# A table set with Exp and Ln loaded by the kernel in a selective scan layer, and two buffers for a norm's row of variances

## The chip, the cores and the metric

The kernel runs on one core of a Trainium2 chip, in one launch. The metric is the device time of the launch in microseconds; a kernel is given by the median of its runs. A profile records one execution with the start and the duration of every instruction. The engines are TensorE (PE, its weight loads as PEld), VectorE (DVE), ScalarE (ACT), GpSimd (POOL) and SyncE (SP), which issues the DMAs. Each takes its own instructions in order.

ScalarE evaluates functions such as Exp, Ln, Silu and Sqrt from tables. The tables come in sets, one set is active at a time, and the instruction that makes another set active shows in the profile as ACT_TABLE_LOAD, under the line of the instruction that it stands in front of.

## The reference

Four layers follow each other on x of shape (8, 64, 64, 64). The change touches the first, a visual state-space block. Cut to what matters, for each of 8 images with 4096 positions and 128 inner channels:

```python
xh = xh + _ss2d(_ln(xh, ...), ...)

def _ss2d(x, ...):
    xi, z = split(x @ in_proj_w.T + in_proj_b)
    xc = silu(_dwconv3(xi, conv_w, conv_b))
    # four directions k: rows, columns, and both reversed
    dts, Bs, Cs = split(xs @ xproj_w)
    dts = softplus(dts @ dtproj_w + dtproj_b)
    # per channel and state n of 16:
    #   h = h * exp(dt * A) + dt * B * u ;  y = sum_n h * C
    y = _ln(y, outnorm_g, outnorm_b) * silu(z)
    return y @ outproj_w.T + outproj_b
```

`_ln` is (x - u) * rsqrt(v + eps) * g + b with mean u and variance v over the channels. The layers after it (a gate with two attentions, a modifier that is trained for two steps, and a last attention) are not changed.

## The kernel before

**Tiling.** Channels lie on the 128 partitions, positions along the free axis. An image is cut into 4 chunks of 1024 positions for the scan (`CH`) and 8 blocks of 512 for everything else (`BK`). `scan_layer` goes over 8 images, and in each over 16 steps: 4 directions times 4 chunks. A step has 16 turns, one for each state n.

**A turn.** The order is written out by hand (a manual schedule), in program order for each engine. For state n, with the work for later states interleaved:

- `decay` (L733, ACT): a = Exp(dt * A_n), two turns ahead, three buffers;
- `spread` (L743 to L754): the row B_n into a PSUM tile z. For 12 of the 16 states PE does it (L751), and DVE multiplies z by dt * u (L778). For the states 0, 3, 6 and 8 (`BY_POOL`) a DMA brings B_n broadcast into `bt`, POOL multiplies (L741), and ACT copies the product to z (L748);
- the scan h = a * h + z on DVE (L782);
- ct = C_n * h on POOL (L787), where ct came by a broadcast DMA (L729, five buffers);
- two turns later, PE adds ct to the sum over n in PSUM (L848); ACT copies the sum of a whole step out (L817);
- ACT copies the last column of h to the state for the next chunk (L769).

**Background work.** Everything that isn't the scan itself stands in a queue of items (`Background`). A turn takes one item: `before` runs its PE half (`make`) and `after`, at the end of the next turn, its other half (`use`), mostly an ACT instruction that empties the PSUM bank. DMAs that such an item ends in are put off to the following turn (`later`). The items: the input norm and projection for the next image, a gate (Silu at L529, 8 blocks for each image), a convolution with Silu (L553, 8 blocks), the step's own projection to dt, B and C (L628, L647, L648), and for the image before it the output norm, the product with the gate and the output projection. In the first four steps of the first image several items are run in one turn, since the convolution there is needed at once.

**Softplus.** log(1 + exp(v)) is computed as Relu(v) + Ln(1 + Exp(-|v|)): Relu (L647) and Abs (L648) out of PSUM, Exp (`soft1`, L653), Ln (`soft2`, L656), and the addition on POOL (`soft3`, L659). In most steps the three stand at the turns 6, 7 and 8.

**The norms.** `inverse_root` turns a row of variances into 1 / sqrt. Its items: for each block a PE product leaves a row of variances in PSUM, and `put` copies it to the SBUF tile `vrow` on ACT (L344) and stores it to DRAM (L345); `fetch` (L352) reads all of them back, spread over the partitions; `root` is the Sqrt (L355), `invert` the reciprocal on DVE (L358) with a store (L359), and `back` (L363) loads the result as the tile `rstd`. `vrow` and `rstd` have one tag, `rstd`, with one buffer. There are 10 such chains on input norms (three for the first image, one for each other) and 11 on output norms (one for each of seven images, four for the last, which is done in pairs of blocks).

**Table loads.** The source before the change has no instruction that loads a table. The compiler puts them in.

Of the kernel before, what the change touches and what calls it, by code (L numbers as in the profile page):

```python
# [10 lines left out]
F32 = mybir.dt.float32  # L11
# [11 lines left out]
BK = 512  # L23
NBK = L // BK
# [217 lines left out]
def scan_layer(cm, x_in, w, xh):  # L242

    tc, nc = cm.tc, cm.nc
    with ExitStack() as ctx:
# [3 lines left out]
        work = ctx.enter_context(tc.tile_pool(name="s_work", bufs=2))  # L249
# [78 lines left out]
        nc.gpsimd.memset(pad, 0.0)  # L328
        bg = Background()

        def bank(name):
            return psum.tile([128, BK], F32, name=name, tag="mm")

# [2 lines left out]
        def inverse_root(nb):  # L336

            var = dr.tile([L], F32, name="vard", tag="vard")[: nb * BK]
            rs = dr.tile([L], F32, name="rsd", tag="rsd")[: nb * BK]
            sm = {}  # L340

            def put(ps, n, at):
                t = work.tile([NBK, BK], F32, name="vrow", tag="rstd", bufs=1)
                nc.scalar.copy(t[:n], ps[:n])  # L344
                bg.later(lambda: nc.sync.dma_start(  # L345
                    var[at * BK : (at + n) * BK].rearrange("(o n) -> o n", o=n), t[:n]
                ))

            def fetch(_):

                sm["v"] = work.tile([128, TQ], F32, name="vsm", tag="vsm")[:, : nb * BK // 128]
                nc.sync.dma_start(sm["v"], var.rearrange("(p f) -> p f", p=128))  # L352

            def root(_):
                nc.scalar.activation(sm["v"], sm["v"], AF.Sqrt, bias=eps)  # L355

            def invert(_):
                nc.vector.reciprocal(sm["v"], sm["v"])  # L358
                bg.later(lambda: nc.sync.dma_start(rs.rearrange("(p f) -> p f", p=128), sm["v"]))  # L359

            def back(_):
                sm["r"] = work.tile([NBK, BK], F32, name="rstd", tag="rstd", bufs=1)[:nb]
                nc.sync.dma_start(sm["r"], rs.rearrange("(j f) -> j f", j=nb))  # L363

            chain = [none, (None, fetch), none, none, (None, root), (None, invert), none]
            chain += [(None, back), none, none, none]
            return put, chain, sm

        def norm_x(b, xn, pairs, project_in):

            put, chain, sm = inverse_root(2 * len(pairs))
            i0, sq = pairs[0], {}

            def centre(i):
                def make():
                    ps = bank("cps")
                    nc.tensor.matmul(ps, ln1_cen, xn[:, i, :], start=True, stop=True)
                    return ps

                def use(ps):  # L380
                    nc.scalar.copy(xn[:, i, :], ps)
                    sq[i] = work.tile([128, BK], F32, name="sq", tag="sq")
                    nc.scalar.activation(sq[i], ps, AF.Square)

                return make, use

            def variance(i):
                def make():
                    ps = bank("vps1")
                    nc.tensor.matmul(ps[:2], ln1_avg, sq.pop(i), start=True, stop=True)  # L390
                    return ps

                return make, lambda ps: put(ps, 2, 2 * (i - i0))

            def apply(i):
                r = 2 * (i - i0)

                def make():
                    ps = bank("rps")
                    rows = ln1_row[: 2 * len(pairs), r : r + 2, :].rearrange("k e c -> k (e c)")  # L400
                    nc.tensor.matmul(ps, rows, sm["r"], start=True, stop=True)
                    return ps

                def use(ps):
                    x = xn[:, i, :]
                    nc.vector.tensor_tensor(x, x, ps, ALU.mult)
                    nc.scalar.activation(x, x, AF.Identity, bias=ln1_b, scale=ln1_g)

                return make, use
# [16 lines left out]
        def norm_y(y, blocks, load, multiply, project_out):  # L426

            put, chain, sm = inverse_root(len(blocks))
            j0, nb, sq = blocks[0], len(blocks), {}

# [58 lines left out]
        def before(b):  # L489

            xn = io.tile([2 * C, NBK // 2, BK], F32, name="xn", tag="xn", bufs=1)

            def block(j):
                e = j % 2
                return slice(e * C, (e + 1) * C), xn[e * C : (e + 1) * C, j // 2, :]
            u = io.tile([DI, L], F32, name="u", tag="u")
            zd = dr.tile([DI, L], F32, name="zd", tag="zd")
            rows = BK // S

            xs = x_in[b].rearrange("c h w -> c (h w)")  # L500

            def load(j):
                return lambda _: nc.sync.dma_start(block(j)[1], xs[:, bass.ts(j, BK)])

            def project_in(j):
                def make():
                    ps = bank("xps")
                    half, x = block(j)
                    nc.tensor.matmul(ps, win[half, 0, :], x, start=True, stop=True)
                    return ps  # L510

                def use(ps):
                    nc.scalar.activation(
                        pad[:, 1 + j * rows : 1 + (j + 1) * rows, 1 : S + 1],
                        ps.rearrange("p (r c) -> p r c", c=S), AF.Identity, bias=inb[:, 0:1],
                    )

                return make, use

            def gate(j):  # L520
                def make():
                    ps = bank("zps")
                    half, x = block(j)
                    nc.tensor.matmul(ps, win[half, 1, :], x, start=True, stop=True)
                    return ps

                def use(ps):
                    z = work.tile([DI, BK], F32, name="z", tag="z", bufs=3)
                    nc.scalar.activation(z, ps, AF.Silu, bias=inb[:, 1:2])  # L529
                    bg.later(lambda: nc.sync.dma_start(zd[:, bass.ts(j, BK)], z))  # L530

                return make, use

            def convolve(j):

                held = []

                def part(t0, t1):
                    def make():
                        if t0 == 0:  # L540
                            held.append(bank("vps"))
                        for t in range(t0, t1):
                            dy, dx = divmod(t, 3)
                            nc.tensor.matmul(  # L544
                                held[0].rearrange("p (r c) -> p r c", c=S), convd[:, t, :],
                                pad[:, j * rows + dy : (j + 1) * rows + dy, dx : dx + S],
                                start=(t == 0), stop=(t == 8),
                            )

                    return make  # L550

                def use(_):
                    nc.scalar.activation(u[:, bass.ts(j, BK)], held[0], AF.Silu, bias=convb)  # L553
                    if b:
                        bg.done[b] += 1

                cuts = (0, 5, 9) if b == 0 else (0, 3, 5, 7, 9) if b == NB - 1 else (0, 2, 4, 6, 8, 9)
                parts = [(part(t0, t1), None) for t0, t1 in zip(cuts, cuts[1:])]
                return parts[:-1] + [(parts[-1][0], use)]

            items = [[(None, load(j)) for j in range(NBK)]]
            for pairs in FIRST if b == 0 else (range(NBK // 2),):
                items.append(norm_x(b, xn, pairs, project_in))
            return u, zd, items, [gate(j) for j in range(NBK)], [convolve(j) for j in range(NBK)]
# [331 lines left out]
        def start(b):  # L896
            u, zd, items, gates, convs = before(b)
            images[b] = {"u": u, "zd": zd}
            bg.add(items[0] + items[1])
            if b == 0:  # L900
                bg.add(convs[0] + convs[1])
                for s in range(1, NCH):
                    later[s] = sum(items[s + 1 : s + 2], []) + convs[2 * s] + convs[2 * s + 1]
                later[NCH] = gates
            else:
                bg.done[b] = 0
                bg.add([(None, lambda _: bg.groups.extend(deque(conv) for conv in convs))])
                bg.add(gates)


        with tc.manual_schedule():
            start(0)
            bg.drain()
            ctl = prepare(0, 0)
# [1243 lines left out]
```

## Time and profile before

| what | us |
|---|---|
| median of 3 runs | 12334.72 (12313.69 to 12336.37) |
| the profiled execution | 12328.75 |
| its span | 12326.7 |
| scan layer, from the start to about | 7053 |
| ACT busy over the span | 7820.8 (63%) |
| DVE busy over the span | 10359.2 (84%) |
| POOL busy over the span | 7399.3 (60%) |
| Exp of `decay`, L733, 2048 of 1147 ns | 2345.4 |
| ACT_TABLE_LOAD, each | 1.283 |
| Silu, L529 and L553, 64 each, of 688 ns | 44.0 and 44.0 |
| Sqrt, L355, 21 of 315 ns | 6.6 |

A group line reads: line, engine, operation, output and input names, shapes, count | busy us, mean ns of one | us that the engine stood idle just before them, and what ended most of it. In a timeline the first two numbers are the start and the duration in us from the start of the span, xN counts instructions that were merged, and in brackets stand the idle time before it and what released it. The page's shares are averages over four layers that have different limits; the scan layer is read by windows of time.

### The profile page before, as it was taken

Reading aid. Unit: us, or ns where it says so; the run is one execution under the profiler, and the core shown is the slowest. Engines: PE = TensorE matmul, PEld = TensorE weight load, DVE = VectorE, ACT = ScalarE, POOL = GpSimd, SP = SyncE. Lnnn points to the kernel's source line nnn. Section 1 sums busy time; section 2 is a strip of 40 time slices with the busy share of each in tenths; the row PEclk is TensorE's granted clock in tenths of the full one; section 3 lists DMA queues with packets and bytes.
Section 4 is the critical chain, followed back from the end, with each engine's and each line's share of the span. In section 5 each row is a group of like instructions: output and inputs, shape, how many; then the busy total and the mean of one; then the engine's idle time right before and its main releaser. Section 6 shows DMA issues by size and latency. Waiting matters only on the chain. (4 is left out here: it accounts for less than half of the span.)

```text
span 12326.7 us, 120038 instructions
## 1 busy us (share of the span) xinstructions
PE 11203.1 (91%) x38827; PEld 4075.9 (33%) x38827; DVE 10359.2 (84%) x7334; ACT 7820.8 (63%) x10409; POOL 7399.3 (60%) x3510
## 2 busy tenths in 40 slices
PE   7899999999999999999998899999987779999999
PEld 2233332332332332333322233232335463333333
DVE  5999999999999999999999776868677686676767
ACT  4776776776766766767766554646547574555554
POOL 5999999999999999999999700000006480000000
PEclk8999999999999999999999899999998789999999
DMA  3666666666666666666666400000011100000000
GB/s 115 207 213 218 209 209 217 219 203 216 218 210 213 211 210 217 213 215 213 199 213 211 164 24 26 5 25 7 17 41 41 41 21 24 19 4 19 5 11 6
DMA packets 541331, 1562.16 MB, mean 127 GB/s; under 512 B 127360, under 2 KB 144400, under 8 KB 538128
## 3 DMA queue, kind: packets, MB, share of 16 engines
q1 hardware_dynamic: 540688, 1554.36, 38.5%
q8 instruction: 309, 5.06, 0.2%
q14 instruction: 334, 2.74, 0.1%
HBM read 1456.41 MB, written 88.87 MB: 125 GB/s over the span
## 5 line engine op out<-in xcount | busy, mean ns | idle before, releaser
L787 POOL TENSOR_TENSOR ct<-ct,h 128x1024 f32<-128x1024 f32 x2048 | 4794.6, 2364 | 248.2 <-DVE h L782 113.3
L782 DVE TENSOR_TENSOR_SCAN h<-a,state,z 128x1024 f32<-128x1024 f32 x1536 | 3573.1, 2342 | 118.2 <-ACT z L748 67.1
L1159 DVE TENSOR_TENSOR sum<-sum,ex 128x1024 f32<-128x1024 f32 x1920 | 2347.5, 1223 | 618.1 <-ACT ex L1152 484.4
L1152 ACT ACTIVATE ex<-sc 128x1024 f32<-128x1024 f32 x2048 | 1968.1, 1024 | 1359.6 <-PE sc L1147 1359.6
L848 PE MATMUL yps<-ct,ident 128*128 128x512 f32 x5632 | 2809.0, 630 | 2.5 <-POOL ct L787 2.4
L733 ACT ACTIVATE a<-dt,amat 128x1024 f32<-128x1024 f32 x2048 | 2345.4, 1147 | 725.9 <-DVE h L782 712.5
L778 DVE TENSOR_TENSOR z<-z,e 128x1024 f32<-128x1024 f32 x1536 | 1863.3, 1213 | 221.1 <-PE z L751 143.2
L1166 PE MATMUL av<-ex,v 128*64 128x512 f32 x8192 | 1950.0, 604 | 0.0
L1147 PE MATMUL sc<-q,k 16*128 16x512 f32 (+1 forms) x8192 | 1562.2, 623 | 4.2 <-ACT q L1140 3.1
L848 PEld LDWEIGHTS yps<-ct,ident 128*128 128x128 f32 x5632 | 1006.4, 194 | 1384.2 <-issue 1220.6
L751 PE MATMUL z<-bs,pick 48*128 48x512 bf16 x3072 | 948.0, 389 | 536.5 <-DVE h L782 485.5
L848 PE MATMUL yps<-ct,lno_cen 128*128 128x512 f32 x2560 | 1276.3, 630 | 0.0
L782 DVE TENSOR_TENSOR_SCAN h<-a,z 128x1024 f32<-128x1024 f32 x512 | 1162.7, 2282 | 81.4 <-ACT z L748 57.2
L741 POOL TENSOR_TENSOR bt<-bt,e 128x1024 f32<-128x1024 f32 x512 | 1210.1, 2364 | 5.3 <-DMA bt<-bc 5.3
L1473 POOL TENSOR_TENSOR gt<-gt,pad 128x1024 f32<-128x1024 f32 x16 | 34.9, 2179 | 1570.2 <-ACT gt L1472 1570.2
L1166 PEld LDWEIGHTS av<-ex,v 128*64 128x64 f32 x8192 | 512.2, 136 | 1332.8 <-issue 1278.9
L1147 PEld LDWEIGHTS sc<-q,k 16*128 16x128 f32 (+1 forms) x8192 | 528.4, 184 | 1016.2 <-issue 977.3
L748 ACT COPY z<-bt 128x1024 f32<-128x1024 f32 x512 | 519.8, 1015 | 537.5 <-POOL bt L741 334.8
L751 PEld LDWEIGHTS <-pick 48*128 48x128 bf16 x3072 | 177.6, 95 | 1754.9 <-DVE h L782 1003.0
L848 PEld LDWEIGHTS yps<-ct,lno_cen 128*128 128x128 f32 x2560 | 458.1, 193 | 618.3 <-issue 564.2
L544 PE MATMUL vps<-pad,convd 128*128 128x512 f32 x1152 | 550.9, 602 | 12.9 <-ACT e L648 12.9
L1846 DVE RECIPROCAL r<-e 128x512 f32<-128x512 f32 x128 | 420.7, 3323 | 0.0
(416 smaller groups left out, 10449.5 us busy)
## 6 DMA issues: line engine op xcount, KB each, us to landing
ct<-bc SPq DMA_DIRECT2D x2048, 512.0 KB
bt<-bc SPq DMA_DIRECT2D x512, 512.0 KB
x<-x SPq DMA_DIRECT2D x12, 2048.0 KB
bc<-e SPq DMA_DIRECT2D x128, 128.0 KB
zd<-z SPq DMA_DIRECT2D x64, 256.0 KB
z<-zd SPq DMA_DIRECT2D x64, 256.0 KB
x<-x SPq DMA_DIRECT2D x32, 512.0 KB
part<-x SPq DMA_DIRECT2D x128, 128.0 KB
```

What stands on the lines that cost most here:

```text
L544: nc.tensor.matmul(held[0].rearrange("p (r c) -> p r c", c=S), convd[:, t, :], pad[:, j * rows + dy : (j + 1) * rows + dy, dx : dx + S], s ...
L733: ctl["exp", n] = nc.scalar.activation(ctl["a", n], ctl["dt"], AF.Exp, scale=amat[:, ctl["k"], n : n + 1])
L741: nc.gpsimd.tensor_tensor(bt, bt, ctl["dus"], ALU.mult)
L751: nc.tensor.matmul(z[:, bass.ts(i, BK)], pick[:, n : n + 1].to_broadcast([3 * N, DI]), ctl["bs"][:, bass.ts(i, BK)], start=True, stop=True,)
L778: first = nc.vector.tensor_tensor(z, z, ctl["dus"], ALU.mult)
L782: nc.vector.tensor_tensor_scan(h[:, flip], a[:, flip], z[:, flip], 0.0 if state is None else state[:, n : n + 1], ALU.mult, ALU.add,)
L787: freed[at] = nc.gpsimd.tensor_tensor(ct, ct, h, ALU.mult)
L848: nc.tensor.matmul(ctl["ps"][:, bass.ts(i, BK)], ctl["mat"], ct[:, bass.ts(i, BK)], start=False, stop=(n == N - 1 and not ctl["turns"]),)
L1147: nc.tensor.matmul(sc[:, e, :], k[r : r + d, bass.ts(j, 128)], qs[i][r : r + d, :], start=True, stop=True,)
L1152: nc.scalar.activation(ex, sc, AF.Exp)
L1159: nc.vector.tensor_tensor(sums[i], sums[i], ex, ALU.add)
L1166: nc.tensor.matmul(avs[i][r, :], v[:, j, r], ex[:, e, :], start=(j == 0), stop=(j == TQ - 1))
```

## The change

`exp_and_ln` is a new function that adds an instruction to ACT's queue that loads the table set with the number 6. It is called once before the schedule begins, behind each Sqrt of `root`, behind each Silu of a gate, and behind each Silu of a convolution. Separately, `vrow` gets a tag of its own with two buffers, so that `rstd` keeps the tag `rstd` with its one buffer for itself.

```diff
+        def exp_and_ln():
+
+            nc.scalar.add_instruction(mybir.InstLoadActFuncSet(
+                name=nc.get_next_instruction_name(), act_func_set_id=6, engine=mybir.EngineType.Activation,
+                ins=[], outs=[],
+            ))
+
...
             def put(ps, n, at):
-                t = work.tile([NBK, BK], F32, name="vrow", tag="rstd", bufs=1)
+                t = work.tile([NBK, BK], F32, name="vrow", tag="vrow", bufs=2)
                 nc.scalar.copy(t[:n], ps[:n])
...
             def root(_):
                 nc.scalar.activation(sm["v"], sm["v"], AF.Sqrt, bias=eps)
+                exp_and_ln()
...
                     nc.scalar.activation(z, ps, AF.Silu, bias=inb[:, 1:2])
+                    exp_and_ln()
                     bg.later(lambda: nc.sync.dma_start(zd[:, bass.ts(j, BK)], z))
...
                     nc.scalar.activation(u[:, bass.ts(j, BK)], held[0], AF.Silu, bias=convb)
+                    exp_and_ln()
                     if b:
                         bg.done[b] += 1
...
         with tc.manual_schedule():
+            exp_and_ln()
             start(0)
```

## The prediction

> **What bounds the kernel now.** I read the page's busy slices first: POOL is at nine tenths or more from the second slice to the 22nd, which is the scan layer, and the chain that ended last names only lines above 1100 for its large shares (attention, modifier). The chain is followed back from the end and keeps few pieces of the scan layer, so I read that layer from its own windows. Columns are busy us (and count) of PE, PEld, DVE, ACT, POOL, then PE clock, DMA share, GB/s:
>
> ```profile
> core 0: us, PE busy (x) PEld busy (x) DVE busy (x) ACT busy (x) POOL busy (x), PEclk, DMA share, GB/s
> 0.00:80.00 80.00, 43.14 (x83) 16.47 (x84) 8.96 (x46) 22.15 (x30) 5.11 (x8) 0.84 0.12 24
> 80.00:300.00 220.00, 177.05 (x394) 62.91 (x393) 140.40 (x80) 127.45 (x176) 145.35 (x67) 0.88 0.44 145
> ...
> 400.00:7000.00 6600.00, 6080.47 (x13893) 2065.63 (x13892) 6301.56 (x3554) 4708.55 (x6745) 6430.62 (x2889) 0.97 0.64 212
> ```
>
> From 400 to 7000 us POOL is busy 6430.6 of 6600 us, DVE 6301.6, ACT 4708.6. So POOL bounds the stage, DVE stands close behind, and ACT, the engine that the change relieves, has 29% to spare. Whatever ACT saves there can return at most POOL's idle time, 6600 - 6430.6 = 169.4 us. Next, the groups on ACT (busy us, mean ns | idle before, and who ended it):
>
> ```profile
> L733 ACT ACT_TABLE_LOAD x266 | 341.3, 1283 | 12.2 <-DVE h L782 7.8
> L656 ACT ACT_TABLE_LOAD x128 | 164.2, 1283 | 2.3
> L529 ACT ACT_TABLE_LOAD x64 | 82.1, 1283 | 1.1
> L553 ACT ACT_TABLE_LOAD x63 | 80.8, 1283 | 1.1
> L344 ACT COPY vrow<-vps 1x512 f32<-1x512 f32 (+1 forms) x96 | 55.0, 573 | 124.8 <-DMA vard<-vrow 108.5 <-PE vps L438 15.2 <-PE vps L390 0.9
> L355 ACT ACT_TABLE_LOAD x21 | 26.9, 1283 | 3.5 <-DMA vsm<-vard 3.2
> ```
>
> With 2 loads at L653 and 1 at L294 (same view) the layer has 545 table loads, 699 us of ACT. The reader is to see two things: every Ln (128 at L656) has a load, and an Exp after it needs another (266 at L733, more than the Silus and roots explain); and the vrow copy waits 108.5 us for its own earlier store, in 27 places. What POOL waits for between 400 and 7000 us (total, times, longest) tells how far this reaches it:
>
> ```profile
> POOL ct L787 <- DMA ct<-bc: 70.7, 81, 4.3
> POOL ct L787 <- DVE h L782: 61.4, 55, 5.1
> ```
>
> Neither is ACT; a slow ACT gets there only through a late DVE or PE. In the timeline the chain of a vrow wait can be seen whole:
>
> ```profile
> 3647.96 0.24 SPq L345 DMA_DIRECT2D vard<-vrow  x1
> ...
> 3650.76 0.58 ACT L344 COPY vrow<-vps 1x512 f32<-1x512 f32 x1 [5.42 <-DMA vard<-vrow]
> ...
> 3653.82 2.35 DVE L782 TENSOR_TENSOR_SCAN h<-a,state,z 128x1024 f32<-128x1024 f32 x1 [4.44 <-ACT z L748]
> ...
> 3656.30 2.35 POOL L787 TENSOR_TENSOR ct<-ct,h 128x1024 f32<-128x1024 f32 x1 [1.42 <-DVE h L782]
> ```
>
> The store was issued late (SP stood at a ct load until 3647.9), ACT stood 5.42 us, DVE 4.44, POOL only 1.42: the lag that POOL carries swallows the rest.
>
> **What the Trainium skill says.** "ScalarE: Activation LUTs", section Table sets: the hidden batching unit, lists a set natural_log_exp_and_others that holds Exp and Ln, so both need one load, and says that relu, copy, identity and abs are in every set. The trace agrees: no Relu, Abs, Copy or Identity has a load in front. The same page, section What ACT_TABLE_LOAD costs, gives 1283 ns for a load and 2.66 us with a drain. The trace has the 1283 ns; the drain isn't seen: after the load at 143.15 us the Exp starts at 144.44. I price a load at 1.29 us. The page also says that a compiler pass puts in a load where one is needed. Whether that pass counts a load that the kernel issues is not said.
>
> **The change, part by part.** Durations are of the profiled execution, 12328.75 us (span 12326.7), 6 below the median of 12334.72.
>
> *Loads.* After it, Exp and Ln need none; each of 64 + 64 Silus and 21 roots has one load in front and one behind, plus one at the start and L294's: 2 x 149 + 2 = 300. So 545 - 300 = 245 go, 314 us of ACT. Beside POOL's 98% nearly all of that is hidden. I walked POOL's idle gaps. Most of the larger ones are led by PE: a convolution's parts and four sum matmul groups in a row (5.42 us) make z late for DVE, with no load in front. Where DVE waited over 0.5 us for ACT and a load that goes stood within 9 us ahead (near 5824, 5829, 5883, 5889, 6883, 6939), POOL lost 0.0 + 0.7 + 0.0 + 0.8 + 2.9 + 1.7 = 6.1 us in the next 10. The bursts near 5829 and 5889 each lose one load of three; this one is typical:
>
> ```profile
> 5880.88 1.28 ACT L733 ACT_TABLE_LOAD   x1
> ...
> 5883.42 1.28 ACT L529 ACT_TABLE_LOAD   x1
> ...
> 5885.42 1.28 ACT L733 ACT_TABLE_LOAD   x1
> ```
>
> The first goes (it follows a Ln), the others stay. PE then stands 3.47 us for the Abs at L648 that frees its bank, and POOL loses 7.2 us at 5904 to 5912; I credit 1.3 of it, the same at 5850, and 3 for places too small to list: 6.1 + 2.6 + 3 = 12 us. Bounds: 4 (the listed ones half recovered) and 75 (of 94 us of POOL idle that has two or more loads in the 14 us before and no vrow wait, four fifths).
>
> *The reload moved.* Behind a Silu it stands at once, not ahead of the next Exp. Read in order, in 15 + 4 = 19 places a z copy (L748) stands between the two; it, and the scan behind it, comes up to 1.28 us later (24 us at worst). In 14 others the bp cast (L698), which waits for POOL, stands between, and the reload now hides in that wait. DVE waits for 34 of 512 z copies, so I take a loss of 1 us net. Two loads in the early steps were behind a copy that waits for PE (142.55, then 143.15 us; again at 221.96) and now fall into that wait, with DVE and POOL waiting behind: 2 x 1.29 = 2.6 us gained.
>
> *Start-up.* POOL stands until 79.27 us, and the chain runs over ACT:
>
> ```profile
> 68.64 0.69 ACT L553 ACTIVATE u<-vps,convb 128x512 f32<-128x512 f32 x1 [7.04 <-PE vps L544]
> 69.65 0.58 ACT L628 COPY e<-dps 64x512 f32<-64x512 f32 x1 [0.31 <-PE dps L619]
> ...
> 74.47 1.28 ACT L653 ACT_TABLE_LOAD   x1
> ...
> 76.84 1.28 ACT L656 ACT_TABLE_LOAD   x1
> ```
>
> The last two go (2.57); the reload at 69.33 pushes the copy at 69.65 back by 1.0; the vrow wait at 33.01 (1.32) goes: 2.9 us.
>
> *Two vrow buffers, and rstd on its own tag.* A store has one more turn (some 3.4 us) to land, so the waits, at most 7.3 us, go or shrink to little. In the 10 us after each wait where DVE then stood for ACT, POOL lost 0.5, 0.3, 1.4, 2.0, 1.8, 1.0, 1.8, 1.3, 0.2: 10.3, rounded up to 11 for the fainter ones. On SP the store keeps its place behind the ct loads; only ACT no longer stands for it, and the next store is ready sooner. Bounds: 5, and 29 (all POOL idle within 20 us after a wait, though the average rate, 0.026 us per us, puts about 13 there anyway). The last norm after the scan has 1.25 us in the open: 1.2. The next layer's first root loses a set that it found loaded; its load falls into ACT's wait for DVE before L151: 0.
>
> Sum: 12 - 1 + 2.6 + 2.9 + 11 + 1.2 = 28.7 us; 12328.75 - 28.7 = 12300, 35 below the median shown (0.28%). What is late next: PE's runs in the convolution steps, and POOL itself.
>
> **Rivals.** *A, ACT's bursts are the root of most POOL gaps* (against it: the gaps led by PE; for it: 94 us with two or more loads before). Then 75 + 29 - 5 us of the steady stage and 6 outside go: about 12225. *B, hidden anyway*: DVE, 95% busy, takes its waits for POOL (44 us) in place of those for ACT, and POOL's gaps move but stay. Only start-up, early steps, the tail and 3 us more return, 10 us: 12319. *C, slower: the pass doesn't count the kernel's loads.* Then 545 stay and 150 come on top, 192 us more of ACT, three loads around a Silu. Such a pile is in the trace once: at 404.93 us DVE stood 6.28 us and POOL lost 5.5. Gate Silus crowd in some 20 steps with 7 to 11 loads; at 5 us each +100, less 15 for vrow: 12414. For it: L733 shows the pass loading by itself; against it: a load is an instruction that such a pass can read. It decides if more than some 11 of those steps lose so much. The weak form of a loss, 19 z copies at full price (24 us), only uses up the forecast's gain.
>
> **How the numbers follow.** Forecast 0.54, A 0.16, B 0.20, C 0.10. About 0.2%, 25 us, can be told from no change here. Faster (below 12310): A, and 0.46 of the forecast's 0.54, makes 0.62; slower: C, 0.10; the rest 0.28. The forecast's own bounds (gains of 10 to 60) give 12269 to 12319; B and the nearer part of A widen it to 12240 to 12328.
>
> **What would show it.** ACT_TABLE_LOAD: none at L656 and L653, about 300 in the layer in place of 545; vrow's wait under 15 us; POOL's start near 76.5; ACT busy down by some 310 us with POOL's idle time from 400 to 7000 still above 120 us. Wrong if loads at L733 stay near 266 (C), if POOL's idle time falls under 90 us (A), or if DVE's wait for z copies grows.

## The result, and the profile after

| | us |
|---|---|
| before, median of 11 runs | 12327.49 (12313.69 to 12355.44) |
| after, median of 11 runs | 12293.15 (12276.48 to 12298.04) |
| ratio, 95% interval | 0.9969 [0.9960, 0.9978] |
| the profiled execution of after, and its span | 12276.48, 12274.4 |

The changed kernel is 0.31% faster by the ratio, 34 us by the medians; 28.7 were predicted for the difference and 12300 for the time. The two profiled executions lie 52 us apart, because that of after is 17 us under its own median: sizes are taken from medians below, and the traces are used to say where a gain sits. Behind the scan layer nothing moved (5274.3 us after, 5273.0 before).

The busy times of after, from the page: engine, busy us, share, instructions.

```profile
PE 11172.2 (91%) x38827; PEld 4068.2 (33%) x38827; DVE 10357.2 (84%) x7334; ACT 7495.1 (61%) x10164; POOL 7396.8 (60%) x3510
```

ACT lost 325.7 us and 245 instructions (10409 before). The groups on ACT in after; the line numbers have moved down by 8 to 11, and L333 is the instruction in `exp_and_ln`:

```profile
L333 ACT ACT_TABLE_LOAD x150 | 192.4, 1283 | 3.3 <-PEq L2156 0.8
...
L562 ACT ACT_TABLE_LOAD x64 | 82.1, 1283 | 1.1
L537 ACT ACT_TABLE_LOAD x64 | 82.1, 1283 | 1.1
...
L351 ACT COPY vrow<-vps 1x512 f32<-1x512 f32 (+1 forms) x96 | 54.8, 570 | 23.1 <-PE vps L446 20.9 <-PE vps L398 1.8
...
L362 ACT ACT_TABLE_LOAD x21 | 26.9, 1283 | 3.3 <-DMA vsm<-vard 3.0
```

These are 299 loads where 545 stood; L294's has become the first of the 150, and one comes on top at the next layer's first root (L151), so that 245 are saved in the whole kernel. The compiler's pass does count what the kernel loads, none is left in front of an Ln or an Exp of the layer, and the vrow copy no longer waits for its own store (108.5 us before).

What POOL and DVE wait for in after, from 400 to 7000 us (total, times, longest):

```profile
DVE z L788 <- PE z L761: 87.1, 89, 3.4
...
POOL ct L797 <- DMA ct<-bc: 61.6, 75, 4.1
...
POOL ct L797 <- DVE h L792: 31.0, 31, 5.1
...
DVE h L792 <- ACT z L758: 16.7, 11, 5.3
```

The last of them in before, of which the prediction gave the number of places, 34, and not the time:

```profile
DVE h L782 <- ACT z L748: 59.5, 34, 6.3
```

POOL's wait for the scan is halved (61.4 before), and the scan's wait for the z copy fell by 43 us. POOL's largest wait, for the ct loads, has PE behind it. In 74 of the 75 places the load was one that SP had held back until PE's sum had read the buffer that it is to fill. SP's waits for these sums, over the stage, most of them early enough to cost POOL nothing:

```profile
SPq L739 <- PE yps L858: 4658.2, 1831, 10.5
```

The busy times of after in stretches (the columns are those of the prediction):

```profile
0.00:80.00 80.00, 42.92 (x83) 16.21 (x84) 9.09 (x46) 25.29 (x34) 7.53 (x10) 0.87 0.12 25
80.00:300.00 220.00, 178.62 (x400) 63.63 (x399) 143.20 (x82) 118.38 (x171) 145.14 (x66) 0.88 0.46 148
...
400.00:7000.00 6600.00, 6092.11 (x13956) 2070.49 (x13955) 6320.40 (x3569) 4405.61 (x6529) 6450.45 (x2903) 0.97 0.64 213
```

ACT is 302.9 us less busy between 400 and 7000. POOL's idle time there is 6600 - 6450.45 = 149.5 us (169.4 before), but the window of after takes in 34 us behind the last scan, in which POOL has little to do. Up to the end of the last scan the trace of before shows

```profile
400.00:7018.60 6618.60, 6096.15 (x13928) 2070.31 (x13926) 6319.99 (x3566) 4715.22 (x6755) 6443.64 (x2895) 0.97 0.64 212
```

and that of after

```profile
400.00:6966.00 6566.00, 6071.08 (x13924) 2065.44 (x13923) 6318.76 (x3566) 4394.97 (x6513) 6439.12 (x2894) 0.97 0.65 213
```

POOL idles 175.0 us in before and 126.9 in after: 48 of the 53 us by which this stretch is shorter are POOL's idle time, as the prediction reckoned. POOL still bounds the stage.

The same vrow place as in the prediction (first output norm of image 4), in the timeline of after:

```profile
3618.82 0.57 ACT L351 COPY vrow<-vps 1x512 f32<-1x512 f32 x1 [0.26 <-PE vps L446]
...
3620.89 9.37 POOL L797 TENSOR_TENSOR ct<-ct,h 128x1024 f32<-128x1024 f32 x4
3621.03 1.02 ACT L758 COPY z<-bt 128x1024 f32<-128x1024 f32 x1 [0.16 <-POOL bt L751]
...
3621.72 0.24 SPq L352 DMA_DIRECT2D vard<-vrow  x1
...
3623.35 2.35 DVE L792 TENSOR_TENSOR_SCAN h<-a,state,z 128x1024 f32<-128x1024 f32 x1 [0.21 <-POOL ct L797]
```

The store is still issued late, 2.9 us after the second vrow copy began, but no one stands for it: 5.42 us of ACT, 4.44 of DVE and 1.42 of POOL are gone, and POOL runs four products in a row.

The start-up in the timeline of after:

```profile
74.11 1.06 ACT L663 ACTIVATE e<-e 128x1024 f32<-128x1024 f32 x1
75.19 1.06 ACT L666 ACTIVATE e<-e 128x1024 f32<-128x1024 f32 x1
...
76.33 2.34 POOL L669 TENSOR_TENSOR dt<-dt,e 128x1024 f32<-128x1024 f32 x1 [71.38 <-ACT e L666]
```

POOL begins at 76.33 and not at 79.27 us, 2.94 earlier; no load stands in front of the Exp or the Ln.

### The profile page after: what moved, and what is told of

It is laid out like the page before. It is cut to its first block, busy times and chain, and to the rows that moved or that the text cites. A ratio compares the mean times of both kernels' runs of the same rounds, so it can differ in the third digit from the quotient of the medians.

```text
span 12274.4 us, 119818 instructions
## 1 busy us (share of the span) xinstructions
PE 11172.2 (91%) x38827; PEld 4068.2 (33%) x38827; DVE 10357.2 (84%) x7334; ACT 7495.1 (61%) x10164; POOL 7396.8 (60%) x3510
```

## The experiments

Three questions were open: how the 34 us divide between the loads and the vrow buffers; within the loads, whether their smaller number or their place counts; and if the place, which one. All kernels were timed against before, with ratio and 95% interval; such an interval is 8 to 17 us to either side, so smaller differences are not told apart. A difference from before is given by the medians of runs timed together, or by the ratio; the two can lie 4 us apart. "Changed" means the kernel of after.

**The loads alone.** The changed kernel with the old line for vrow:

```diff
-                t = work.tile([NBK, BK], F32, name="vrow", tag="vrow", bufs=2)
+                t = work.tile([NBK, BK], F32, name="vrow", tag="rstd", bufs=1)
```

> The table loads of the change alone; the row of variances keeps its one buffer, shared with rstd. Theory both (the prediction's): the loads give about half of the 34 us, 15 to 22 us, ratio to before 0.9982 to 0.9988, the vrow waits stay at about 108 us, and the gain lies in the steps with gates and convolutions. Theory loads alone: 30 us or more, ratio 0.9975 or less. Theory vrow alone: under 6 us, ratio above 0.9995, and about 300 loads in the scan layer in place of 545 all the same.

12316.83 us (21 runs), ratio 0.9986 [0.9980, 0.9993]: 15.3 us under before. The scan's wait for the z copy stays at 55.9 us in this trace.

**The vrow buffers alone.** The kernel before with that one line of the change:

```diff
-                t = work.tile([NBK, BK], F32, name="vrow", tag="rstd", bufs=1)
+                t = work.tile([NBK, BK], F32, name="vrow", tag="vrow", bufs=2)
```

> The two buffers alone; all loads as before. Theory both: 12 to 20 us, ratio 0.9984 to 0.9990, vrow's wait for its store under 10 us, gain in the norm's steps only. Theory loads alone: under 6 us. Theory vrow alone: 30 us or more. If the two parts hide each other, the sum of this gain and that of the loads alone differs from 34 us by more than 10.

12314.87 us, ratio 0.9985 [0.9977, 0.9993]: 17.3 us. The two add up, 15.3 + 17.3 = 32.6 of 34 us. The waits from 400 to 7000 us in its trace:

```profile
POOL ct L787 <- DMA ct<-bc: 78.5, 95, 4.2
POOL ct L787 <- DVE h L782: 37.4, 40, 5.0
...
DVE h L782 <- ACT z L748: 19.8, 22, 6.3
```

This edit alone takes the scan's wait for the z copy from 59.5 to 19.8 us and POOL's for the scan from 61.4 to 37.4; 8 us come back as waits for ct loads. The gain can be placed in the traces by comparing the start of every scan with before: the lead is how much earlier a scan starts. In the step that works on an output norm (step 1 of an image) the lead jumps within one scan, right behind the place where ACT had stood: by 3.4 us at the wait of 5.42 us above, by 3.2 at one of 7.3 us in the same step. Over images 1 to 6 these jumps come to 26.7 us in step 1 and 12.2 in step 6 (the input norm); 8.4 and 6.0 of it are given back in the steps behind. So about 4 us per image stay.

**The loads at their old place.** The changed kernel, with the reload put directly in front of the next Exp or Ln, where the compiler had it:

```diff
                     nc.scalar.activation(z, ps, AF.Silu, bias=inb[:, 1:2])
-                    exp_and_ln()
+                    leave()
...
             def soft1(_=None):
+                exp_and_ln()
                 nc.scalar.activation(e, e, AF.Exp, scale=-1.0)
```

The same stands at the convolution's Silu, the root, `soft2` and `decay`; `leave` sets a flag, and `exp_and_ln` loads when it is set.

> The change, but the reload stands directly ahead of the next Exp or Ln, as the compiler had it, and not behind the Silu or the root. If the place of the reload is worth nothing (prediction: a loss of 1 us and 2.6 us gained early), this is within 6 us of the changed kernel, ratio to before 0.9965 to 0.9975. If the 19 z copies behind a reload cost their full 1.28 us, this is 15 to 25 us faster than the changed kernel. If the reload's hiding in waits is what gained, it is 10 us or more slower.

12311.45 us, ratio 0.9983 [0.9975, 0.9991]: 18 us slower than the changed kernel by the medians, 17 by the ratios, 14 if each is taken from its own runs of before; the two intervals just touch. Against the vrow buffers alone (0.9985) the fewer loads bring 3 us, which is not told from none. So beside two vrow buffers nearly all that the loads bring hangs on the place.

**Fewer loads alone.** The same with one vrow buffer, so that the kernel before has only loads taken away (250, since a reload that nothing needs is left out too):

```diff
-                t = work.tile([NBK, BK], F32, name="vrow", tag="vrow", bufs=2)
+                t = work.tile([NBK, BK], F32, name="vrow", tag="rstd", bufs=1)
...
-                    exp_and_ln()
+                    leave()
```

> The loads in front of Ln and the reloads behind it go (set of Exp and Ln), but the reload behind a Silu or a root stands directly ahead of the next Exp, and the row of variances keeps its one buffer. Theory place (the reload's place behind the Silu is what gains): 0 to 6 us faster than before, ratio 0.9995 to 1.0000. Theory count (245 fewer loads are what gains): 12 us or more, ratio 0.9990 or less.

12322.96 us, ratio 0.9993 [0.9985, 1.0002]: 9 us by the ratio and 12 by the medians, not told from none, and not from "the loads alone" either.

**The place alone.** A set with Exp but without Ln, loaded where the changed kernel loads its set, and one vrow buffer. The loads around each Ln stay:

```diff
-                name=nc.get_next_instruction_name(), act_func_set_id=6, engine=mybir.EngineType.Activation,
+                name=nc.get_next_instruction_name(), act_func_set_id=0, engine=mybir.EngineType.Activation,
```

> The set with Exp alone is loaded behind each Silu and root, so that Ln and the Exp behind it have their loads as before, some 545 in the layer; the row of variances keeps its one buffer. Theory place: 10 to 16 us faster than before, ratio 0.9987 to 0.9992. Theory count: within 4 us of before.

12318.66 us, ratio 0.9989 [0.9982, 0.9995]: 14 us by the ratio, 16 by the medians. The groups of its loads:

```profile
L333 ACT ACT_TABLE_LOAD x150 | 192.4, 1283 | 3.3 <-PEq L2156 0.8
...
L666 ACT ACT_TABLE_LOAD x128 | 164.2, 1283 | 2.2
L743 ACT ACT_TABLE_LOAD x128 | 164.2, 1283 | 2.3
```

With the 64 + 64 + 21 in front of Silus and roots, 555 loads stand here, ten more than before the change, and the time is that of "the loads alone" (by the medians 16 and 15 us under before). So the place gains with no load fewer, and on top of it no gain of the number is seen, though some 10 us of it can't be excluded.

The number without the place is less clear: 9 to 12 us with one vrow buffer, 3 with two. The runs tell more when their clock is taken in. Each run has a granted clock, the mean TensorE clock of the run as a share of full speed, and over 94 runs of before the time falls by some 7 us for each 0.001 of it (correlation -0.88). A straight line for the clock through the runs of all kernels, with a level for each kernel, gives an estimate of the gains at equal clock, in us under before, each to some 3 or 4 us either way:

| kernel | us |
|---|---|
| one vrow buffer: fewer loads alone; place alone; loads alone | 10; 12; 12 |
| two: vrow alone; loads at their old place; changed | 22; 21; 34 |

Thus with one vrow buffer the number seems to gain as well, and number and place stand in for each other; with two, the number adds nothing and the place 13. Why the number counts only beside the vrow waits is open, and so is whether the kernel itself moves the clock.

**Which place.** Read in order on ACT, 88 of the 128 Silus have an Exp right behind them; there both places are the same. In 14 the bp cast stands between (ACT's rounding to bf16 of a difference that POOL makes just before, for the rows of B), in 19 a z copy. 28 of these 33 are in steps 9 and 10 of an image, where the gate's Silus run. First the timeline of the kernel with the reload late (image 3, steps 10 and 11; L718 is the bp cast, L754 `decay`, L666 the Abs, L799 DVE's product, L808 POOL's):

```profile
3287.07 0.40 ACT L718 CAST bp<-br 128x256 bf16<-128x256 f32 x1 [3.02 <-POOL br L715]
...
3287.49 1.28 ACT L341 ACT_TABLE_LOAD   x1
...
3288.79 1.15 ACT L754 ACTIVATE a<-dt,amat 128x1024 f32<-128x1024 f32 x1
...
3313.69 3.49 PE L561 MATMUL vps<-pad,convd 128*128 128x512 f32 x4 [1.59 <-ACT e L666]
...
3319.76 1.23 DVE L799 TENSOR_TENSOR z<-z,e 128x1024 f32<-128x1024 f32 x1 [2.49 <-PE z L772]
...
3332.93 4.69 POOL L808 TENSOR_TENSOR ct<-ct,h 128x1024 f32<-128x1024 f32 x2 [2.13 <-DVE h L803]
```

And the same places in after:

```profile
3267.13 1.28 ACT L333 ACT_TABLE_LOAD   x1
...
3270.05 0.41 ACT L708 CAST bp<-br 128x256 bf16<-128x256 f32 x1 [1.63 <-POOL br L705]
...
3270.36 1.15 ACT L743 ACTIVATE a<-dt,amat 128x1024 f32<-128x1024 f32 x1
...
3295.48 1.99 PE L553 MATMUL vps<-pad,convd 128*128 128x512 f32 x4 [0.75 <-ACT e L658]
...
3299.85 1.23 DVE L788 TENSOR_TENSOR z<-z,e 128x1024 f32<-128x1024 f32 x1
...
3312.99 2.35 POOL L797 TENSOR_TENSOR ct<-ct,h 128x1024 f32<-128x1024 f32 x1 [0.68 <-DVE h L792]
```

Here the load runs while ACT would stand for POOL anyway: the wait in front of the cast shrinks from 3.02 to 1.63 us, and the Exp follows the cast at once. ACT carries the 1.3 us through the burst of Silus; the Abs comes earlier, frees PE's bank earlier, PE's convolution stands 0.75 and not 1.59 us, DVE's wait of 2.49 us for z is gone, and POOL's of 2.13 us has become 0.68. The order of these is in the traces; that each brings about the next is my reading. It is the same point of an image, the Abs in step 11, at which the prediction saw PE stand near 5890.

The lead over before that is gained in step 11, over images 1 to 6 (from the starts of the scans, one trace for each kernel), is the clean mark of it:

| kernel | us |
|---|---|
| changed; loads alone; place alone | 12.8; 12.7; 12.7 |
| loads at their old place; fewer loads alone; vrow alone | 0.8; 2.0; -0.1 |
| late at the bp casts; late at the z copies | 6.9; 5.0 |
| late in the first image only | 12.6 |

The last three lines come from these kernels. **Late at the bp casts:** the gate's reload is issued as the next turn begins, so behind a bp cast but still ahead of a z copy.

```diff
                     nc.scalar.activation(z, ps, AF.Silu, bias=inb[:, 1:2])
-                    exp_and_ln()
+                    leave()
...
                     for n in range(N):
+                        exp_and_ln()
                         empty()
```

> The change, but the reload behind a gate's Silu is issued at the start of the next turn, so that in the 14 places where the bp cast follows it stands behind the cast's wait for POOL, and not in it; all else as in the changed kernel. If hiding in that wait is what the place is worth, 8 us or more of the 14 to 18 that the reload ahead of the next Exp cost are lost: 12301 us or more, ratio 0.9976 to 0.9983. If the z copies are what counts, within 4 us of the changed kernel, ratio 0.9966 to 0.9973.

12296.13 us (7 runs), ratio 0.9969 [0.9958, 0.9980], not told from the changed kernel. **Late at the z copies:** `leave` loads at once unless a z copy comes next.

```diff
+        def leave():
+            stale[0] = True
+            if not defer[0]:
+                exp_and_ln()
...
+                        defer[0] = (n + 2) % N in BY_POOL and not early
```

> The changed kernel, with the reload put behind the z copy in the places where a z copy follows the Silu (19 of 128), and right behind the Silu everywhere else, the bp-cast places included. The changed kernel stands 34 us under before; with all reloads ahead of the next Exp or Ln it lost 18 of it. Theory 1, the reload hides in the z copy's wait for POOL: this kernel loses most of that, 12 to 18 us, and comes out at a ratio of about 0.9983. Theory 2, it is the bp cast's wait: nothing is lost, ratio about 0.9970, and the wait of DVE for z in step 11 stays gone. Theory 3, the two kinds of places stand in for each other, or the loss comes from the first image: 0 to 6 us are lost.

12307.77 us (9 runs), ratio 0.9978 [0.9968, 0.9987]: 11 us of the 34 lost by the ratios, in an interval that overlaps the changed kernel's. By the medians the z copies carry more than the bp casts; by step 11 each carries about half (6 and 8 of 12 us). Both kinds of place count in the traces, and at equal clock, estimated as above, the kernels late at one kind lose 8 and 11 us (each to some 5), where all loads at their old place lose 13; their shares of the time are left open. **The first image:**

```diff
+                        defer[0] = b == 0
```

> The changed kernel, with the reload ahead of the next Exp or Ln in the start-up and the first image, and right behind the Silu in the seven others. If the early steps, in which several convolutions stand in one turn, carry what the late reload lost, this kernel is 5 to 18 us slower than the changed one (ratio 0.9973 to 0.9984); if the loss is spread over the images, one in eight of it is lost, 2 us, which cannot be told from the changed kernel (ratio about 0.9970).

12297.97 us (8 runs), ratio 0.9972 [0.9961, 0.9982], 4 us above the changed kernel by the ratios and 5 by the medians, not told from it. The early steps are not where most of the reload's place counts.

**More of the same.** If fewer loads or fewer waits on ACT were still worth something, the next two should show it. The root as Exp(-0.5 Ln(v + eps)), with 42 loads and DVE's reciprocal gone:

```diff
-                nc.scalar.activation(sm["v"], sm["v"], AF.Sqrt, bias=eps)
-                exp_and_ln()
+                nc.scalar.activation(sm["v"], sm["v"], AF.Ln, bias=eps)
+                nc.scalar.activation(sm["v"], sm["v"], AF.Exp, scale=-0.5)
```

> The change, but 1/sqrt(v + eps) is computed as Exp(-0.5 Ln(v + eps)) on ACT in the set that is loaded, so that the 21 roots need no table load in front or behind and DVE no reciprocal: 42 loads fewer. If loads cost where they stand in the norm's chain, 5 to 15 us faster than the changed kernel; if they lie in slack, within 5 us of it.

12285.57 us (5 runs), ratio 0.9963 [0.9949, 0.9977], 8 us under the changed kernel by the medians, not told from it.

The bp cast, for which ACT stands 235.2 us in after, with fetch, first cast and subtraction one turn earlier:

```diff
+                            if len(do) > 1:
+                                for i in range(3):
+                                    hooks[6 + i] = [do[i]]
+                                del hooks[9]
```

> The changed kernel with the pieces fetch, first and subtract one turn earlier, so that POOL has one turn more before ACT's bp cast needs its difference. ACT's wait for POOL at that cast, about 200 us in all, should fall below 80. If such waits of ACT cost time, 10 to 25 us faster than the changed kernel, ratio to before 0.995 to 0.996; if they are slack, within 5 us of it.

12289.01 us (5 runs), ratio 0.9961 [0.9947, 0.9974]. Its group of the cast:

```profile
L708 ACT CAST bp<-br 128x256 bf16<-128x256 f32 x64 | 25.6, 400 | 35.7 <-POOL br L705 35.5
```

200 us of ACT's waiting at this cast are gone and 4 us of time, if any: most of these waits were slack. Both edits together:

> The changed kernel with the root by Exp and Ln (42 table loads fewer) and with the cast of B one turn later, together. Each alone stood 4 to 8 us under the changed kernel, no more than two such measurements differ by. If both gains are real they add: about 12281, ratio 0.9957. If neither is, this comes out at 0.9970 like the changed kernel.

12292.55 us (5 runs), ratio 0.9961 [0.9947, 0.9974]. The gains do not add, so neither is shown; no version here is told from the changed kernel.

## Why the prediction was right, and which terms were not

The time, 12293 against 12300, and the direction are right, and so is the frame: POOL bounds the layer, and what was saved is its idle time. Two sums inside it came out by luck, with wrong parts.

- **The number of loads.** Right: 245 fewer, with ACT's busy time down by 326 us. The open question of the pass, rival C, is answered by the first view of the profile: it counts the kernel's loads. Rival A is out: up to the last scan POOL kept 126.9 us of idle time, above the 120 named, though not by much. B is out with 34 us gained.
- **"Loads", 12 us, and "the reload moved", -1.** Together with start-up and early steps the prediction had 12 - 1 + 2.6 + 2.9 = 16.5 us for this part, and the loads alone measured 15.3. But the prediction gave the number 12 and the place -1, and the parts stand otherwise: that the sum fits is luck. Beside two vrow buffers, taking 250 loads away without moving any gave 3 us and the place 14 to 18 more. With one, the number alone gave 9 to 12 with an interval that holds zero, and the place alone 14 to 16 with no load fewer. The step that failed is the sentence that weighed 19 delayed z copies against 14 hidden reloads and came to "a loss of 1 us net". It feared for the z copy. That copy does come about 1 us later, but part of the load hides there too, since the copy stood waiting for POOL: its mean wait is 0.32 us with the reload late and 0.04 us in after, and from the end of the Silu to the Exp it takes 2.63 and 2.29 us. The scan's wait for z copies, the sign that was named, did not grow (22.5 us with the reload late, 16.7 in after). At the bp casts the time from Silu to Exp is 4.54 and 3.12 us.
- **"The first goes (it follows a Ln)"**, of the burst near 5889. The burst was rightly picked, as step 11 of an image, but misread: what stands in front of the load at 5880.88 in the trace of before is a convolution's Silu (5878.29) and the copy of `ut`. That load doesn't go, it moves, and the same holds near 5829, where the load at 5821.55 follows a convolution's Silu. What freed PE earlier in such places came from the reloads of the gate's Silus a step ahead. The 7.2 us of POOL behind it are, in the trace, three waits for ct loads (4.33, 0.96 and 1.87 us), and each of these loads was issued right behind a PE sum that SP stood for (10.4, 3.1 and 3.8 us): the path from PE to POOL there runs over the ct buffers. (POOL's 98% is 6430.6 of 6600, 97.4%.)
- **Early steps, 2.6 us.** Not seen. After the start-up's gain of 3.6 us at the first scan, the trace of after stands 0.8 us behind before at step 8, and a late reload in the whole first image cost 4 to 5 us, not told from none.
- **Start-up, 2.9.** The trace of after has 2.94, but only half of it is shown. From the second Silu to POOL's start it takes 10.63 us in before and 9.05 in after: these 1.58 us are the two loads less the reload (2.57 - 1.0). The other 1.36 lie ahead of that Silu and are not the vrow wait, or not surely: ACT's idle time there only fell from 1.32 to 0.64 us (now for PE), the loads alone, which keep that wait whole, let POOL start at 76.19, and the vrow buffers alone, which keep both loads, at 77.05. The start-up differs by such amounts from trace to trace.
- **Two vrow buffers, 11, and the tail, 1.2.** The mechanism is right, the size is not: 17.3 us for 12.2, within the bound of 29. The mis-sized term is what POOL lost "in the 10 us after each wait", 10.3 us over nine places. At the place shown, that counted POOL's 1.42 us, while the scans came 3.4 us earlier once the wait was gone. DVE is 95% busy behind POOL, so I read it thus that what DVE loses in 4.44 us reaches POOL later too, outside the 10 us, and isn't swallowed by POOL's lag. The scan's wait for the z copy fell by 39.7 us; less the 14.4 that come back in the steps behind it is 25. In that trace the lead at the last scan is 22.2 us, the medians give 17.3: this measure comes out too high where POOL's loss in 10 us came out too low. The tail, from the last scan to the end of the layer, fell from 35.0 to 34.1 us.

"ScalarE: Activation LUTs", section What ACT_TABLE_LOAD costs, in the Trainium skill gives 2.66 us with a drain; no trace here shows it. In after a gate's Silu ends at 3274.72, the load behind it starts at 3274.73 and the Exp at 3276.03: a switch costs 1.31 us with all around it.

## What to carry to other kernels

On an engine that takes its instructions in order, ask of each unavoidable stall (a table load) what stands between its cause and its need: put it where the engine would wait for another engine anyway. Beside two vrow buffers that was worth 14 to 18 us, where removing 45% of the loads brought 3. And where two engines are nearly full, don't price a wait only by what the bounding engine loses in the few microseconds behind it: look also at the delay of the first engine that it reaches, and count what stays, since a part is given back in the next steps. Here the one gave 10 us and the other 25, and the gain, 17, lay between.

## What the hardware showed that was not expected

- The compiler's pass takes a load that the kernel issues into account: 150 instructions put in by hand left 149 of the pass's 545 in the layer, with none doubled.
- 555 loads run as fast as 299 (16 and 15 us under before by the medians, with the same placing behind Silus and one vrow buffer): the 328 us of ACT between them cost nothing that could be measured, to some 10 us, in a layer where ACT is 71% busy.
- Two bp casts and two z copies in steps 9 and 10 of an image, with some 1.4 and 0.3 us hidden at each, made step 11 shorter by 2.1 us (12.8 over six images, and 0.8 with the reload late): the effect shows up to two steps behind its cause, and in the timeline it seems to pass through a PSUM bank that PE gets back earlier.
- POOL's largest wait, 61.6 us for ct loads, is PE's lateness in another form: in 74 of 75 places SP had held the load back until PE's sum had read the buffer.
